# Combining row minima and row sums of attention with an operand per partition on VectorE

## The chip, the cores and the metric

The kernel runs on one core of a Trainium2 chip. The metric is the device time of one execution in microseconds (us); lower is better. Before the change the median of three runs is 3795.2 us (3794.46 to 3797.17).

The core's engines are called by short names: PE is TensorE (matrix products), DVE is VectorE, ACT is ScalarE, POOL is GpSimd, SP is SyncE, whose queue issues nearly all the DMAs. SBUF is the on-chip working memory of 128 partitions, PSUM the memory that PE writes its products to.

## The reference, cut to what matters

Four images of 384 channels and 32 x 32 pixels pass through two layers in fp32. The first is a group normalisation, a selective state-space scan in four directions (16 states for each channel and direction), a layer normalisation and a GELU, added to the image. The second sees the image as 1024 tokens of 384 channels: causal attention with one head, and then a mixture of four experts, of which each token uses two. The change lies in the softmax of the attention:

```python
q = jnp.einsum('btc,ch->bth', x, Wq)
k = jnp.einsum('btc,ch->bth', x, Wk)
v = jnp.einsum('btc,ch->bth', x, Wv)
wei = jnp.einsum('bth,bsh->bts', q, k) * scale
wei = jnp.where(causal, wei, -jnp.inf)
wei = jax.nn.softmax(wei, axis=-1)
out = jnp.einsum('bts,bsh->bth', wei, v)
```

## The kernel before, in words

**Scans.** The scan of an image is cut into 192 units (768 in all, L558 to L571). A unit has 32 channels with 4 states each on the 128 partitions and the 1024 pixels along the free dimension. It takes an exponential `da` on ACT (`decay`, L551), a product `v` on DVE (`front`, L558: `du` and `bc`, both in SBUF, into PSUM), a scan on DVE (`middle`, L564: `da` in SBUF and `v` in PSUM, into `h`), and a product on POOL (`back`, L571: `h` times `bc`, all in SBUF). After every fourth unit PE sums the states (`row`, L596).

**The order of the work.** The kernel is one Python loop over ticks, one unit a tick, which writes the instructions into each engine's queue in a fixed order. In tick t it calls, in this order: `decay` of unit t+2, the deferred functions that are due, `front` of unit t, `back` of unit t-1, the deferred functions of the kind "inner", `middle` (the scan) of unit t, `row`, the fetches, the preparation of the next image and a step of the image before, which is in attention or in the experts. `back` is given a dependence on the `front` of the same tick, so that POOL's product starts once that product of DVE is done, and lies beside the scan.

**Attention.** It runs for image b while the scans of image b+1 go on; for the last image nothing is scanned beside it. For each block i of 128 tokens (8 blocks in an image), `scores` (L925, and L930 for the causal mask) computes the negated scores of the 128 tokens against all tokens up to the block's end on PE. A row of up to 512 scores lies in one PSUM bank. A longer row (i of 4 to 7) has two parts in two banks.

`softmax` is deferred to the "inner" place of a later tick, between `front` and the scan on DVE. It takes the minimum of each part into a column of the small tile `nb` (L939, 48 in all). If there are two parts, it combines their minima into `nb[:, 0:1]` (L941, 16 in all, 4 an image). ACT then takes the exponentials of each part with that minimum as bias, and adds them up into `nb[:, 2:3]` and `nb[:, 3:4]` (L943). `normalise` comes in the next tick, among the functions that are due, ahead of `front`: with two parts it adds the two sums (L953, 16 in all), takes the reciprocal (L954) and lets ACT scale the row (L955). After that, `turn` transposes the row on PE (L970) and copies it with ACT (L887), and `values` multiplies it with the values (L988, L991) and copies the result (L1003).

Other lines that the text speaks of: L339 and L340 in `groupnorm` scale three means and three variances per partition with `tensor_scalar` and a constant, from SBUF to SBUF; L371 normalises 1024 pixels with `tensor_scalar` and two operands per partition, the second of which L368 has just written; L1216 in the experts is a `scalar_tensor_tensor` on DVE with one tensor in PSUM, one in SBUF and an operand per partition in SBUF; L1074 in `gates` adds a constant to four sums.

Of the kernel before, what the change touches and what calls it, by code (L numbers as in the profile page):

```python
# [10 lines left out]
ALU = mybir.AluOpType  # L11
# [38 lines left out]
def hybrid_kernel(  # L50
# [22 lines left out]
    nc = tc.nc  # L73
# [41 lines left out]
    def defer(ticks, f, where=due):  # L115
        where.setdefault(clock[0] + ticks, []).append(f)
# [752 lines left out]
    def attention(b, yb, fx0):  # L869
# [49 lines left out]
        def scores(i):  # L919
            ss = []  # L920
            for o in range(0, (i + 1) * P, 512):
                e = min((i + 1) * P, o + 512)
                ps = yield from banks.take(f"ss_{b}_{i}_{o}")
                for c in range(M):
                    nc.tensor.matmul(  # L925
                        ps[:, : e - o], qt[:, c, i * P : (i + 1) * P], xn[:, c, o:e],
                        start=(c == 0), stop=(c == M - 1 and e <= i * P),
                    )
                if e > i * P:
                    nc.tensor.matmul(ps[:, e - o - P : e - o], ident, causal, start=False, stop=True)  # L930
                ss.append((o, e, ps[:, : e - o]))
                yield "pe", 2.6 * (e - o) / 512
            pr = prs[i] = yield from slots.take(f"pr_{b}_{i}", P, L)
            defer(1, lambda: softmax(i, ss, pr), inner)

        def softmax(i, ss, pr):
            nb = sm.tile([P, 4], F32, tag="nb", name=f"nb_{b}_{i}")
            for n, (o, e, ps) in enumerate(ss):
                nc.vector.tensor_reduce(nb[:, n : n + 1], ps, AX.X, ALU.min)  # L939
            if len(ss) == 2:  # L940
                nc.vector.tensor_tensor(nb[:, 0:1], nb[:, 0:1], nb[:, 1:2], ALU.min)  # L941
            for n, (o, e, ps) in enumerate(ss):
                nc.scalar.activation(  # L943
                    pr[:, o:e], ps, AF.Exp, bias=nb[:, 0:1], scale=-1.0,
                    accum_out=nb[:, 2 + n : 3 + n],
                )
                banks.give(f"ss_{b}_{i}_{o}")
            defer(1, lambda: normalise(i, nb, len(ss)))

        def normalise(i, nb, n):  # L950
            wd = (i + 1) * P
            if n == 2:
                nc.vector.tensor_add(nb[:, 2:3], nb[:, 2:3], nb[:, 3:4])  # L953
            nc.vector.reciprocal(nb[:, 2:3], nb[:, 2:3])  # L954
            nc.scalar.activation(prs[i][:, :wd], prs[i][:, :wd], AF.Copy, scale=nb[:, 2:3])  # L955

# [442 lines left out]
```

## Time and profile before

| | |
|---|---|
| median of three runs | 3795.2 us (3794.46 to 3797.17) |
| profiled execution, its own time | 3795.0 us |
| span of the profile | 3793.2 us |
| mean granted clock of PE | 0.927 |
| PE busy | 3366.5 us, 89% of the span |
| DVE busy | 2964.4 us, 78% |
| ACT busy | 2089.9 us, 55% |
| POOL busy | 1815.1 us, 48% |

The profile is that of one execution. Each engine's busy time counts from an instruction's start to its end as the profiler saw them, so that a wait after the start counts as busy. The granted clock is the share of its full clock that PE was given. In a timeline a row has the start in us from the span's start, the duration in us, the engine, the line of the kernel, the operation, what is written and read by the program's names, the shape per instruction and the count; in brackets stands how long the engine was idle before it, and what ended that. A row that counts more than one instruction merges them, and its duration is then that of the whole stretch. The chain of work that ended last is followed back from the end of the span: at each step to what released the instruction, or to the one ahead of it on its engine.

The work of one image takes about a quarter of the span, shifted so that scans of one image lie beside attention and experts of the one before. The 16 instructions of L941 lie at 821 to 859 us, 1659 to 1704, 2481 to 2520 and 3229 to 3255, four in each stretch. In the last stretch POOL has no work.

### The profile page before, as it was taken

What the parts mean: (1) busy time and instruction counts of PE and PEld (TensorE: products, weight loads), DVE (VectorE), ACT (ScalarE), POOL (GpSimd) and SP (SyncE); (2) the same over time, 40 slices, a digit from 0 to 9 for tenths busy, and PEclk for the clock granted to TensorE, in tenths of its full rate; (3) what the DMA queues carried; (4) which work ended last, traced back from release to release, by engine and by line L of the source; (5) the groups of instructions that cost most, each with busy time, mean ns of one, the idle gap of its engine ahead of it and who ended that gap; (6) DMA issues with size and microseconds to landing.
All of it is one profiled execution on the core that took longest, in us unless ns stands there. A gap on an engine that the chain in (4) does not pass through costs nothing.

```text
span 3793.2 us, 34275 instructions
## 1 busy us (share of the span) xinstructions
PE 3366.5 (89%) x11543; PEld 1518.3 (40%) x11543; DVE 2964.4 (78%) x2084; ACT 2089.9 (55%) x2767; POOL 1815.1 (48%) x776
## 2 busy tenths in 40 slices
PE   4666666689999999799999999889999999999999
PEld 1333333245333334345333343354343434644444
DVE  6899899998889999989998999999999982210000
ACT  5888888555656656556655555455554552422121
POOL 2777777554455556445555565455665550000000
PEclk7767877799999999898999999899999999999999
DMA  6655655635576767336666565345656551222321
GB/s 207 218 209 219 220 199 208 230 122 184 191 245 208 255 205 251 140 136 225 215 221 223 197 212 185 143 167 195 215 194 237 180 182 38 91 78 80 96 83 53
DMA packets 407983, 678.80 MB, mean 179 GB/s; under 512 B 33488, under 2 KB 280576, under 8 KB 407808
## 3 DMA queue, kind: packets, MB, share of 16 engines
q1 hardware_dynamic: 401600, 676.22, 52.0%
q8 instruction: 91, 1.49, 0.2%
q10 hardware_dynamic: 6208, 0.39, 0.1%
q14 instruction: 84, 0.69, 0.1%
HBM read 604.57 MB, written 71.96 MB: 178 GB/s over the span
## 4 chain that ended last, share of the span: by engine, by line
DVE 42%; PE 40%; ACT 7%; issue 6%; DMA 3%; POOL 1%; DVEq 0%; SPq 0%; POOLq 0%; ACTq 0%
DVE h L564 25%; PE ph L1182 13%; PE fy L1207 13%; DVE v L558 12%; PE y L596 4%; ACT da L551 2%; PE ss L925 2%; PE pq L896 2%; PE pv L907 2%; PE v L841 1%; PE pxd L391 1%; ACT st L819 1%; DVE du L438 1%; DMA du<-dts 1%; PE po L991 1%
## 5 line engine op out<-in xcount | busy, mean ns | idle before, releaser
L571 POOL TENSOR_TENSOR h<-h,bc 128x1024 f32<-128x1024 f32 x768 | 1814.0, 2366 | 1308.6 <-DVE v L558 1142.8
L564 DVE TENSOR_TENSOR_SCAN h<-da,v 128x1024 f32<-128x1024 f32 x768 | 1750.5, 2284 | 104.4 <-PE v L841 29.7
L551 ACT ACTIVATE da<-dt,a 128x1024 f32<-128x1024 f32 x768 | 883.3, 1156 | 923.7 <-DVE h L564 887.2
L1182 PE MATMUL ph<-fx,w 128*128 128x512 f32 x2304 | 1024.8, 601 | 6.5 <-ACT dt L430 2.3
L1207 PE MATMUL fy<-ht,w 128*128 128x512 f32 x2304 | 1021.2, 600 | 1.5 <-ACT dt L430 0.9
L558 DVE TENSOR_TENSOR v<-du,bc 128x1024 f32<-128x1024 f32 x678 | 841.7, 1241 | 38.8 <-DMA du<-dts 21.7
L1182 PEld LDWEIGHTS ph<-fx,w 128*128 128x128 f32 x2304 | 434.9, 192 | 583.4 <-issue 528.9
L1207 PEld LDWEIGHTS fy<-ht,w 128*128 128x128 f32 x2304 | 436.8, 192 | 574.9 <-issue 552.2
L596 PE MATMUL y<-h,sel 128*32 128x512 f32 x3072 | 493.8, 661 | 101.4 <-POOL h L571 101.3
L1167 ACT ACTIVATE ht<-ph,b1s 128x512 f32<-128x512 f32 x384 | 257.2, 678 | 459.5 <-PE ph L1182 459.1
L1216 DVE SCALAR_TENSOR_TENSOR fy<-fy,b2s,tw 128x512 f32<-128x512 f32 x96 | 72.4, 754 | 425.8 <-PE fy L1207 425.8
L596 PEld LDWEIGHTS y<-h,sel 128*32 128x32 f32 x3072 | 97.4, 116 | 412.2 <-issue 219.8
L841 PE MATMUL v<-ident,st 128*128 128x128 f32 x720 | 143.1, 364 | 110.6 <-DVE h L564 110.6
L819 ACT ACTIVATE st<-turn,bt 128x128 f32<-128x128 f32 x736 | 213.6, 532 | 0.1
L841 PEld LDWEIGHTS v<-ident,st 128*128 128x128 f32 x720 | 115.4, 189 | 155.6 <-DVE h L564 78.3
L1171 ACT ACTIVATE ht<-ht 128x3072 f32<-128x3072 f32 x64 | 176.9, 2763 | 0.8
L551 ACT ACT_TABLE_LOAD x108 | 138.6, 1283 | 13.8 <-DMA dt<-dts 11.9
L991 PE MATMUL po<-pt,vt 128*128 128x256 f32 x480 | 105.4, 368 | 9.4 <-ACT pt L887 9.4
L424 PE MATMUL pdt<-xd,wdt 12*128 12x512 f32 x184 | 81.0, 762 | 34.8 <-ACT dt L430 19.4
L925 PE MATMUL ss<-axn,qt 128*128 128x512 f32 (+3 forms) x288 | 106.1, 514 | 0.8 <-ACT pr L943 0.5
L991 PEld LDWEIGHTS po<-pt,vt 128*128 128x128 f32 x480 | 93.1, 195 | 24.9 <-ACT pt L887 12.0
L939 DVE TENSOR_REDUCE nb<-ss 128x1 f32<-128x512 f32 (+3 forms) x48 | 26.1, 554 | 78.8 <-PE ss L930 63.5
(200 smaller groups left out, 1661.7 us busy)
## 6 DMA issues: line engine op xcount, KB each, us to landing
bc<-rows SPq DMA_DIRECT2D x384, 512.0 KB, 4.9
w<-in_w SPq DMA_DIRECT2D x384, 384.0 KB, 6.1
dt<-dts SPq DMA_DIRECT2D x192, 512.0 KB, 3.8
du<-dts SPq DMA_DIRECT2D x192, 512.0 KB, 6.7
dts<-dt SPq DMA_DIRECT2D x48, 512.0 KB, 5.3
dts<-du SPq DMA_DIRECT2D x48, 512.0 KB, 3.8
fx<-t2d SPq DMA_DIRECT2D x12, 768.0 KB, 5.3
tw<-mkd SPq DMA_DIRECT2D x32, 256.0 KB, 6.3
```

Of the source, the lines that this page charges most:

```text
L551: nc.scalar.activation(u["da"], spread["dt4", n], AF.Exp, scale=a4[:, g, u["q"] : u["q"] + 1])
L558: return nc.vector.tensor_tensor(u["v"], spread["du4", n], spread["bc", n][:, 0, :], ALU.mult)
L564: nc.vector.tensor_tensor_scan(u["h"][:, ::step], u["da"][:, ::step], u["v"][:, ::step], 0.0, op0=ALU.mult, op1=ALU.add,)
L571: product = nc.gpsimd.tensor_tensor(h, h, spread["bc", n][:, 1, :], ALU.mult)
L596: nc.tensor.matmul(y, sel, h, start=first, stop=last, tile_position=(0, jj * DJ))
L819: nc.scalar.activation(st[:, 4 * h + t, :].rearrange("p (d i) -> p i d", i=NI)[:, i, :], ps[h][:, t * P : (t + 1) * P], AF.Copy, scale=bt[ ...
L841: nc.tensor.transpose(u["v"][:, t * P : (t + 1) * P], st[:, t, u["j"] * P : (u["j"] + 1) * P], ident)
L925: nc.tensor.matmul(ps[:, : e - o], qt[:, c, i * P : (i + 1) * P], xn[:, c, o:e], start=(c == 0), stop=(c == M - 1 and e <= i * P),)
L991: nc.tensor.matmul(pv[:, o:], vt[:, j, m * P : (m + 1) * P], pts[step][j // 4][:, j % 4, o:], start=False, stop=(j == nj - 1),)
L1167: nc.scalar.activation(ht[:, f, :], ps, AF.Identity, bias=bias)
L1182: nc.tensor.matmul(ps, tiles[n][:, c, (f % 2) * P : (f % 2 + 1) * P], xns[h][:, c, :], start=(c == 0), stop=(c == M - 1),)
L1207: nc.tensor.matmul(pss[m], tiles[n][:, f, :], hts[fh][:, f, :], start=(fh == 0 and f == 0), stop=(fh == 1 and f == FH - 1),)
```

## The change

In `softmax`, the tensor_tensor that takes the smaller of two minima becomes a tensor_scalar: its one tensor is the first minimum, and the second comes in as an operand per partition. In `normalise`, the tensor_tensor that adds the two sums becomes a tensor_scalar in the same way. Operands, result and the place in the order stay the same.

```diff
             if len(ss) == 2:
-                nc.vector.tensor_tensor(nb[:, 0:1], nb[:, 0:1], nb[:, 1:2], ALU.min)
+                nc.vector.tensor_scalar_min(nb[:, 0:1], nb[:, 0:1], nb[:, 1:2])
...
             if n == 2:
-                nc.vector.tensor_add(nb[:, 2:3], nb[:, 2:3], nb[:, 3:4])
+                nc.vector.tensor_scalar_add(nb[:, 2:3], nb[:, 2:3], nb[:, 3:4])
```

## The prediction

> **What bounds the kernel now.** I read the chain of work that ended last first, to see which engine a saved microsecond must come from.
>
> ```profile
> DVE 42%; PE 40%; ACT 7%; issue 6%; DMA 3%; POOL 1%; DVEq 0%; SPq 0%; POOLq 0%; ACTq 0%
> ```
>
> VectorE (DVE) and TensorE (PE) carry the end in turn. From 800 to 3160 us, where attention and experts of one image lie beside the scans of the next, DVE is 92% busy (2176.6 of 2360 us) and PE 95%, so a stall of either is likely to count. Second, the groups of instructions by form, for the two lines that are changed (columns: instructions, busy us and mean ns, idle before).
>
> ```profile
> L941 DVE TENSOR_TENSOR nb<-nb 128x1 f32<-128x1 f32 x16 | 11.4, 712 | 0.6
> ...
> L953 DVE TENSOR_TENSOR nb<-nb 128x1 f32<-128x1 f32 x16 | 2.2, 140 | 5.4 <-ACT pr L943 5.4
> ```
>
> The same shape of operation costs 140 ns at L953 and 712 ns at L941. The single instructions of L941 run from 159 to 1711 ns with a median of 182, so a few long ones make the mean. Third, the timeline around one long one (start, us, engine, line).
>
> ```profile
> 839.03 2.34 POOL L571 TENSOR_TENSOR h<-h,bc 128x1024 f32<-128x1024 f32 x1 [1.26 <-DVE v L558]
> ...
> 839.96 1.44 DVE L941 TENSOR_TENSOR nb<-nb 128x1 f32<-128x1 f32 x1
> 841.32 2.27 DVE L564 TENSOR_TENSOR_SCAN h<-da,v 128x1024 f32<-128x1024 f32 x1
> ```
>
> GpSimd's (POOL's) product ends at 839.03 + 2.34 = 841.37; L941 ends at 841.40. In all seven instances of 0.67 us and more (at 830.02, 839.96, 1659.29, 1684.69, 2481.16, 2491.08 and 2501.05) it ends within 0.03 us of the end of the product under way. One comparison per partition takes 160 ns where no product is under way, so most of those 1.44 us are a wait for POOL, booked as busy. Fourth, is that wait on the path? The chain in order of time, same place:
>
> ```profile
> 838.87 1.07 DVE nb L939 x2
> 839.93 0.02 issue
> 839.96 1.44 DVE nb L941
> 841.40 2.20 DVE h L564
> ```
>
> The chain passes through it, as through the other six. Nothing hides it.
>
> **What the Trainium skill says.** "GPSIMD Engine Reference", section "Key points", says that POOL shares its SBUF interfaces with VectorE, and that it contends with DVE instructions in a 2-port performance mode or with two SBUF inputs. The trace agrees for two inputs: L941 reads both from SBUF and waits, while L1216 (one SBUF tensor, one in PSUM, one operand per partition from SBUF) takes 0.75 us at 1001.29 inside a product that runs from 1000.36 to 1002.72, its usual time of 754 ns. So an operand per partition, as such, doesn't wait. "VectorE: DVE Perf Modes", section "The perf-mode tier table", gives fp32 tensor_scalar in SBUF the 2x mode, which uses both ports. The trace agrees: L371 handles 1024 elements in 811 ns, where L558 takes 1241 for the same width. "Vector Engine (DVE) Microarchitecture Reference", section 5.1, ties that mode to SBUF operands whose outermost dimension over one is even, or equal on both sides. What one element per partition does it doesn't say, and no row of this trace shows a tensor_scalar of one element. "TensorE: Matmul & The Clock Gate", section "What's actually happening", says that PE falls to half clock after an idle window of about 3.4 us; the trace agrees, with a granted clock of 0.50 from 2508.6 to 2512.2, after 3.40 us of idle.
>
> **The change, part by part.**
>
> Removed: 16 tensor_tensor at L941, 11.4 us. Added: 16 tensor_scalar with an operand per partition, in the same place of the same queue. No DMA, tile or wait on another engine is added, and POOL's and SP's queues are untouched. Undisturbed instances of L941 take 159 to 163 ns. The nearest rows for the new form are L339 and L340 (tensor_scalar, 128x3), 136 to 154 ns undisturbed, and L1074 (128x4), 170 ns. So the bare operation changes by -0.02 to +0.01 us, and 16 of them by -0.4 to +0.2 us. I take 0. Reading as an operand per partition what the instruction in front has just written adds no gap that I can see: L371 starts 0.04 us after L368, which writes its operand, as L941 starts 0.03 us after L939.
>
> The wait is the open cost. 11.4 us less 16 x 0.160 = 2.6 us leaves **8.8 us**. At one end the new form doesn't contend, and all 8.8 us are gone; at the other it contends as before, and nothing is. The row that argues for the latter is L339, where it meets the end of a product:
>
> ```profile
> 1415.47 2.35 POOL L571 TENSOR_TENSOR h<-h,bc 128x1024 f32<-128x1024 f32 x1 [1.34 <-DVE v L558]
> 1417.63 0.20 DVE L339 TENSOR_SCALAR gn_mc<-gn_mc 128x3 f32<-128x3 f32 x1
> ```
>
> It takes 205 instead of 136 ns and ends at 1417.83, as the product ends (1417.82); so a tensor_scalar of three elements does wait. What one element does rests on whether a single element is split over two ports. There is nothing to split, so I take, narrowly, that it isn't and that the wait goes.
>
> L953 -> tensor_scalar_add: its 16 instances take 126 to 160 ns, none meets a product, the new form costs the same by the rows above; 0. Its cover is that it comes right behind a scan, when the product that ran beside that scan is over. With L941 faster, the product still started before the scan and ends before it (831.57 against about 832.4 at the first place), so the cover stays. Without it, one sum could wait up to 2.35 us.
>
> What is late next, if the 8.8 us go? Behind L941 on DVE stands the scan L564; on ACT the exponentials L943 wait for it, and behind them `da`, the copies and PE's transposes. At the first image (1.41 + 1.28 = 2.7 us) the chain comes to PE here (PE's timeline, idle before it in brackets):
>
> ```profile
> 849.24 0.48 PE L970 MATMUL tp<-ident,pr 128*128 128x128 f32 x1 [4.53 <-ACT yb L1003]
> ```
>
> PE sat idle for 4.53 us, more than 2.7, so it takes the whole gain. At the second image, 0.5 us meet idle of 0.88 (1666.85), and 1.28 us meet 3.40 (1692.28). At the third, 1.55 + 1.48 + 1.28 = 4.3 us meet 3.40 at 2508.63; PE's work ahead of that can itself move up by its own waits of 0.33 and 0.56, so some 4.2 pass. That makes 2.7 + 0.5 + 1.3 + 4.2 = 8.7 us. Afterwards all engines have moved alike, so the shift stays to the end; the last image's four instances (3229 to 3254) have no product beside them, and change by 0.
>
> A second gain comes from PE's clock. The gaps at 849, 1692 and 2508 are followed by about 6 us at half clock (12 matmuls of L925 take 8.0 us at 849.7, and 5.15 at 3248 where the clock is full), so 3 us each. In the shorter gaps (about 2.9, 2.6 and under 0.5 us) the fall is likely avoided at the third and about evenly open at the other two. But DVE waits for those scores by only 1.23, 1.03 and 1.11 us (before L939 at 857.99, 1702.71 and 2518.78), and no more than that can be had: 0.5 x 1.2 + 0.5 x 1.0 + 0.9 x 1.1 = 2.1 us. Small losses, where PE has less slack than I see, I put at 0.8 us.
>
> Sum against the profiled execution: span 3793.2 - 8.7 - 2.1 + 0.8 = 3783.2 us; with the 1.8 us around the span (3795.0 - 3793.2) 3785.0. Its time stands 0.2 us under the median of the three runs, 3795.2, which is less than their spread of 2.7.
>
> **The rivals.**
>
> The wait stays. The single element runs in the two-port mode after all, and L941 ends with the product, as before. For it: L339. Against it: one element has no second half. Nothing moves: 3795.0 us, 3793.5 to 3797.
>
> The wait goes, and PE's clock takes it back; this one ends slower. DVE frees the scores earlier, PE runs ahead, and gaps that are now just short of a fall grow past it: 2.21 us before 1708.55, 2.21 before 2524.61, 2.79 before 2539.15. Each fall costs about 3 us (6 us at half clock). It decides from the third fall that is new: 3795.0 - 8.7 + 3 x 3 = 3795.3, and with a fourth 3798.3. Against it: the gaps after the waits shrink, since PE waits for DVE there, and the stages after them move as a whole.
>
> The change does not do what it says: if both forms came out as the same instruction, the profile would show TENSOR_TENSOR at L941 again, and the time is that of the first rival. I count it there.
>
> **How the numbers follow.** The wait goes: 0.52, 3785 us, own range 3781 to 3789. The wait stays: 0.41, 3795. Clock takes it back: 0.07, about 3798. The first two hold most of the chance, so the range reaches from 3782 to 3797. A measurement of this kernel can tell about 0.2%, that is 7.6 us, from no change; the line is 3787.6. Four fifths of the first case lie below it: 0.42 faster. The rest of the first case (0.10), the second and 0.04 of the third are within 0.2%: 0.55. Slower by more: 0.03, the part of the third with more falls than the four counted.
>
> **What would show it.** Right: a TENSOR_SCALAR at L941 with 16 instances near 160 ns, the longest under 0.25 us, though a product runs; DVE's busy time down by about 9 us; the idle before PE's L970 (849) and L596 (1692, 2508) shorter. Wrong in the second way: the longest instance is still about 1.7 us and ends with a product. Wrong in the third: L941 is short, and PE's granted clock falls in stretches where it is full now. My forecast fails if one element does take both ports.

## The result, and the profile after

The changed kernel takes 3781.2 us (median of 8 runs, 3779.65 to 3789.62), against 3796.2 (8 runs, 3790.32 to 3803.41, the three shown first among them) for the kernel before. The ratio is 0.9968 with a 95% interval of 0.9959 to 0.9977: 12.1 us less, between 8.7 and 15.6. The two medians lie 15.0 us apart, which is within that interval. The median of the changed kernel lies 0.8 us under the forecast's range.

The profiled execution of the changed kernel has a span of 3777.9 us. The chain's shares first:

```profile
DVE 41%; PE 40%; ACT 7%; issue 7%; DMA 3%; POOL 1%; DVEq 0%; SPq 0%; POOLq 0%; ACTq 0%
```

DVE and PE still carry the end in turn; no other engine has become the bound. The two changed lines in the groups by form:

```profile
L941 DVE TENSOR_SCALAR nb<-nb 128x1 f32<-128x1 f32 x16 | 3.4, 214 | 0.6
...
L953 DVE TENSOR_SCALAR nb<-nb 128x1 f32<-128x1 f32 x16 | 3.2, 200 | 5.8 <-ACT pr L943 5.8
```

L941 went from 11.4 to 3.4 us and is now even: its 16 instances take 213 to 215 ns. L953 went from 2.2 to 3.2 us. DVE's busy time fell from 2964.4 to 2956.2 us. The timeline at the place that the prediction showed:

```profile
837.49 2.35 POOL L571 TENSOR_TENSOR h<-h,bc 128x1024 f32<-128x1024 f32 x1 [1.26 <-DVE v L558]
838.41 0.21 DVE L941 TENSOR_SCALAR nb<-nb 128x1 f32<-128x1 f32 x1
838.54 2.28 DVE L564 TENSOR_TENSOR_SCAN h<-da,v 128x1024 f32<-128x1024 f32 x1
```

The product runs until 839.84, and the minimum is done at 838.62 all the same; the scan starts 1.3 us before the product ends. On the chain in order of time the piece shrank from 1.44 to 0.21 us, with the same neighbours:

```profile
837.32 1.07 DVE nb L939 x2
838.39 0.03 issue
838.41 0.21 DVE nb L941
838.62 2.19 DVE h L564
```

**Where the time came from.** I measured three attention stages by DVE's scans, counted from 1 to 768: from the start of scan 223 to that of 230, of 413 to 425, and of 607 to 617. They hold all the waits. Each figure is from one execution, the profiled one. In the kernel before they last 30.9, 59.4 and 48.0 us; in the changed one 28.5, 55.8 and 42.9. That is 2.4 + 3.6 + 5.1 = 11.1 us less. The two profiled spans differ by 15.3. The other 4.2 us lie outside the three stages, where the changed kernel spends 3650.6 us and the kernel before 3654.9. Of the kernels below, those that keep the waits spend 3654.5 to 3661.9 us there, and those that lose them 3653.1 to 3662.7: single executions differ by more than 4.2 us there, so this part isn't shown to be the change's. 11.1 us fit the ratio's 12.1.

### The profile page after: what moved, and what is told of

Read it like the earlier page. It is cut to its first block, busy times and chain, and to the rows that moved or that the text cites. A ratio compares the mean times of both kernels' runs of the same rounds, so it can differ in the third digit from the quotient of the medians.

```text
span 3777.9 us, 34275 instructions
## 1 busy us (share of the span) xinstructions
PE 3355.5 (89%) x11543; PEld 1511.6 (40%) x11543; DVE 2956.2 (78%) x2084; ACT 2089.8 (55%) x2767; POOL 1815.2 (48%) x776
## 4 chain that ended last, share of the span: by engine, by line
DVE 41%; PE 40%; ACT 7%; issue 7%; DMA 3%; POOL 1%; DVEq 0%; SPq 0%; POOLq 0%; ACTq 0%
DVE h L564 25%; PE ph L1182 14%; PE fy L1207 13%; DVE v L558 13%; PE y L596 4%; ACT da L551 2%; PE pq L896 2%; PE pv L907 2%; PE v L841 1%; DMA du<-dts 1%; PE ss L925 1%; PE pxd L391 1%; PE po L991 1%; DVE du L438 1%; DVE fy L1216 1%
## 5 line engine op out<-in xcount | busy, mean ns | idle before, releaser
L551 ACT ACT_TABLE_LOAD x108 | 138.6, 1283 | 13.3 <-DMA dt<-dts 11.4
```

The lines of the kernel that those rows point to most:

```text
L551: nc.scalar.activation(u["da"], spread["dt4", n], AF.Exp, scale=a4[:, g, u["q"] : u["q"] + 1])
```

## Experiments

The three stages as above, and the ratio to the kernel before, for all kernels:

| kernel | stage 1, us | stage 2, us | stage 3, us | ratio (95% interval) |
|---|---|---|---|---|
| before | 30.9 | 59.4 | 48.0 | 1 |
| changed | 28.5 | 55.8 | 42.9 | 0.9968 (0.9959 to 0.9977) |
| min_only | 28.3 | 56.7 | 42.7 | 0.9967 (0.9954 to 0.9979) |
| sum_only | 31.0 | 59.4 | 48.2 | 1.0000 (0.9992 to 1.0008) |
| two_elements | 30.9 | 59.2 | 48.1 | 0.9998 (0.9990 to 1.0006) |
| min_then_idle | 30.9 | 58.4 | 48.1 | 1.0001 (0.9993 to 1.0009) |
| min_then_free | 28.5 | 57.0 | 43.2 | 0.9973 (0.9965 to 0.9981) |
| psum_second | 28.2 | 57.4 | 43.7 | 0.9976 (0.9968 to 0.9984) |
| third_image | 30.9 | 58.7 | 42.7 | 0.9988 (0.9982 to 0.9995) |
| const_sum | 28.3 | 56.7 | 42.7 | one run, 3786.2 us |
| filled_gap | 30.9 | 61.7 | 51.6 | 1.0018 (1.0010 to 1.0025) |
| min_filled | 28.3 | 61.9 | 42.7 | 0.9987 (0.9980 to 0.9995) |
| filled_zero | 30.9 | 59.1 | 48.0 | 1.0000 (0.9992 to 1.0009) |
| min_filled_zero | 28.3 | 55.3 | 42.7 | 0.9966 (0.9954 to 0.9978) |

My theory: a tensor_tensor with both inputs in SBUF can't run while POOL's product does, a tensor_scalar of a single element can, and the scan behind it carries the gain. Rivals: the new form as such is faster, wherever it stands; the gain comes from the exponentials, not from the scan; a value per partition never waits, whatever the number of elements.

**Each half alone: min_only and sum_only.**

```diff
 min_only
-                nc.vector.tensor_tensor(nb[:, 0:1], nb[:, 0:1], nb[:, 1:2], ALU.min)
+                nc.vector.tensor_scalar_min(nb[:, 0:1], nb[:, 0:1], nb[:, 1:2])
 sum_only
-                nc.vector.tensor_add(nb[:, 2:3], nb[:, 2:3], nb[:, 3:4])
+                nc.vector.tensor_scalar_add(nb[:, 2:3], nb[:, 2:3], nb[:, 3:4])
```

> Only the minimum (L941) takes its second value per partition; the sum stays a tensor_tensor. If the wait for GpSimd's product at L941 is the whole cause, L941 takes 0.21 us in all 16 instances and the time is that of the full change, ratio 0.997 to the kernel before, less about 0.05 us for each of 16 sums. If the sum has a share in the gain, the ratio lies between 0.997 and 1.

> Only the sum (L953) takes its second value per partition. If L941's wait is the cause, nothing is gained: L941 keeps its seven instances of 0.6 to 1.7 us, each sum takes 0.19 instead of 0.13 us, and the time is 0 to 1 us above the kernel before, ratio 1.000. If the new form itself is what helps, it falls by some microseconds.

The minimum alone gives the whole gain; the sum alone gives none. With the sum alone, the groups by form read:

```profile
L941 DVE TENSOR_TENSOR nb<-nb 128x1 f32<-128x1 f32 x16 | 11.6, 723 | 0.5
...
L953 DVE TENSOR_SCALAR nb<-nb 128x1 f32<-128x1 f32 x16 | 3.1, 195 | 5.4 <-ACT pr L943 5.4
```

The sum takes 195 instead of 140 ns, and no more is to be had, since nothing waits at L953. The new form as such is slower, not faster: the first rival falls.

**One element or two: two_elements.** The minimum is taken over both columns, so the second column comes out as it was.

```diff
-                nc.vector.tensor_tensor(nb[:, 0:1], nb[:, 0:1], nb[:, 1:2], ALU.min)
+                nc.vector.tensor_scalar_min(nb[:, 0:2], nb[:, 0:2], nb[:, 1:2])
```

> The minimum takes its second value per partition, but over both columns of the tile (two elements per partition; the second comes out unchanged). The sum stays. If one element escapes because it can't be split over two ports, two elements are split, and L941 waits for the product again: up to 1.7 us, ratio 1.000. If a value per partition never waits, L941 takes 0.21 us and the ratio is 0.997.

```profile
842.82 2.34 POOL L571 TENSOR_TENSOR h<-h,bc 128x1024 f32<-128x1024 f32 x1 [1.26 <-DVE v L558]
843.74 1.44 DVE L941 TENSOR_SCALAR nb<-nb 128x2 f32<-128x2 f32 x1
845.10 2.27 DVE L564 TENSOR_TENSOR_SCAN h<-da,v 128x1024 f32<-128x1024 f32 x1
```

The timeline at the same place shows the wait again: it ends at 845.18, and the product at 845.16. The operation, the operand per partition and the place are those of the changed kernel; only the second element is new. So the wait goes because of the single element, not because of the operand per partition alone. This is the step that the prediction left to a guess. The reading, which no run shows directly, is that one element isn't handled in the mode that needs both ports. It agrees with the Trainium skill, "Vector Engine (DVE) Microarchitecture Reference", section 5.1: by the rule there, two elements from SBUF to SBUF with one source take the mode with both ports, as an even count does; of one element the page says nothing.

**The scan or the exponentials, which both wait for the minimum: min_then_idle and min_then_free.** An instruction whose result nobody reads stands behind the new minimum and ahead of the scan, once in each form.

```diff
+    junk = const.tile([P, 1], F32, tag="junk", name="junk")
...
-                nc.vector.tensor_tensor(nb[:, 0:1], nb[:, 0:1], nb[:, 1:2], ALU.min)
+                nc.vector.tensor_scalar_min(nb[:, 0:1], nb[:, 0:1], nb[:, 1:2])
+                nc.vector.tensor_tensor(junk, eps, eps, ALU.min)      # min_then_idle
+                nc.vector.tensor_scalar_min(junk, eps, eps)           # min_then_free
```

> The minimum as in the changed kernel, and behind it a tensor_tensor of one element with two SBUF inputs, whose result nobody reads. It should wait for the product in the place of L941, up to 1.7 us, and hold the scan behind it, but not ScalarE's exponentials. If the scan's delay carries the loss, the time is that of the kernel before (ratio 1.000); if the exponentials' delay carries it, that of the changed kernel (0.997).

> As the kernel with an idle tensor_tensor behind the new minimum, but that instruction too is a tensor_scalar of one element with its second value per partition. It is the control for the bare cost of one more instruction in that place: 16 x 0.2 us at most, so a ratio of 0.997 to 0.998. If one more instruction on DVE in this place is by itself what loses the gain, it is 1.000.

The timeline of min_then_idle (its lines count one further, two behind the edit):

```profile
841.23 2.35 POOL L572 TENSOR_TENSOR h<-h,bc 128x1024 f32<-128x1024 f32 x1 [1.26 <-DVE v L559]
842.15 0.21 DVE L942 TENSOR_SCALAR nb<-nb 128x1 f32<-128x1 f32 x1
842.28 1.32 DVE L943 TENSOR_TENSOR junk<-eps 128x1 f32<-128x1 f32 x1
842.40 0.69 ACT L945 ACTIVATE pr<-ss,nb 128x512 f32<-128x512 f32 x1 [1.46 <-DVE nb L942]
...
843.52 2.27 DVE L565 TENSOR_TENSOR_SCAN h<-da,v 128x1024 f32<-128x1024 f32 x1
```

The exponentials start at 842.40, right behind the minimum, as in the changed kernel. The idle instruction ends at 843.60, and the product at 843.58. The scan behind it starts at 843.52; here as in the kernel before and in the changed one, its start lies 0.08 us ahead of the end of the instruction in front. The gain is gone: ratio 1.0001. In the other form the instruction costs 204 ns, and the ratio stays at 0.9973. So what counts is the scan's delay. The wait needs no dependence on anything: both inputs are one constant tile.

**Another way around the wait: psum_second.** The tensor_tensor stays; for blocks 4 to 6 the second minimum goes to the free last column of its PSUM bank.

```diff
             for n, (o, e, ps) in enumerate(ss):
-                nc.vector.tensor_reduce(nb[:, n : n + 1], ps, AX.X, ALU.min)
+                low = nb[:, n : n + 1] if n == 0 or spare_ is None else spare_
+                nc.vector.tensor_reduce(low, ps, AX.X, ALU.min)
             if len(ss) == 2:
-                nc.vector.tensor_tensor(nb[:, 0:1], nb[:, 0:1], nb[:, 1:2], ALU.min)
+                nc.vector.tensor_tensor(nb[:, 0:1], nb[:, 0:1], low, ALU.min)
```

`spare_` is column 511 of the second part's bank for blocks 4 to 6, and None for block 7, whose bank is full.

> The minimum stays a tensor_tensor, but for the blocks 4 to 6 of an image the second part's minimum is written to the free last column of its PSUM bank, so that only one of the two inputs lies in SBUF. If two SBUF inputs are what waits, the twelve instances of blocks 4 to 6 take about 0.2 us beside a product and the ratio is about 0.997, a little behind the changed kernel [...]. If any tensor_tensor waits, it stays at 1.000.

The groups by form (the first line is block 7, the second blocks 4 to 6):

```profile
L943 DVE TENSOR_TENSOR nb<-nb 128x1 f32<-128x1 f32 x4 | 2.8, 708 | 0.1
...
L943 DVE TENSOR_TENSOR nb<-nb,ss 128x1 f32<-128x1 f32 x12 | 1.9, 155 | 0.4
```

With one input in PSUM none of the twelve waits, so two SBUF inputs are the cause. They take 155 ns, no more than the undisturbed 159 to 163 with both inputs in SBUF. But the ratio is only 0.9976, and the stages 2 and 3 gain less than with the new form. The reason is in the first line: the minimum of block 7, which didn't wait in the kernel before, now does. It takes 1.09 us in the second stage and 1.30 in the third, and in each of them the last two scans of the stage (423 to 425, 615 to 617) take 11.2 us instead of min_only's 10.1. The wait has moved.

**One stage alone: third_image.** The new minimum for the third image, the old one for the others (`if b == 2`).

> Only the third image's four minima take their second value per partition. By the working of the prediction this stage gains 4.2 us from the waits and about 1.0 us from PE's clock, and the other stages nothing: the stretch of the third attention is 5.2 us shorter, and the ratio is about 0.9986. If the shift didn't stay to the end, or the gain lay elsewhere, the ratio would be 1.000.

The third stage takes 42.7 us, 5.3 less, and the first one is as before; the second is 0.7 shorter, within what it varies by among kernels with its waits (58.4 to 59.4; why it varies is seen further down). The ratio is 0.9988, where 5.3 of 3796 us are 0.9986. The gain stays to the end.

**What the operand per partition costs: const_sum.** The minimum in the new form, and the sum with a constant.

```diff
-                nc.vector.tensor_add(nb[:, 2:3], nb[:, 2:3], nb[:, 3:4])
+                nc.vector.tensor_scalar_add(nb[:, 2:3], nb[:, 2:3], 1.0)
```

> The minimum as in the changed kernel; the sum adds a constant in place of the second sum (which is left out, so the weights of long rows are not normalised rightly). If the value per partition is what makes the new form take 0.19 to 0.21 us, L953 takes about 0.13 us here; if it is tensor_scalar as such, 0.19 us.

```profile
L953 DVE TENSOR_SCALAR nb<-nb 128x1 f32<-128x1 f32 x16 | 2.2, 138 | 3.4 <-ACT pr L943 3.4
```

By the groups by form, the sum takes 138 ns with a constant and 195 to 200 with an operand per partition (sum_only and the changed kernel): the operand costs about 60 ns an instruction.

**The share of PE's clock: filled_gap and min_filled, then filled_zero and min_filled_zero.** In the second and third stage PE is idle for 3.4 us until POOL's last product is there, and its clock falls to half for 6.8 us, from 0.8 and 1.4 us before PE starts again. Three matmuls in that gap should keep it up. In the first attempt they wrote to a bank for scores:

```diff
+                if n in (419, 611) and half == 0 and jj == NJ - 1 and banks.ready():
+                    fill = bank("fill")
+                    for _ in range(3):
+                        nc.tensor.matmul(fill, ident, ybs[b - 1][:, 0, :512], start=True, stop=True)
                 nc.tensor.matmul(
                     y, sel, h, start=first, stop=last, tile_position=(0, jj * DJ)
                 )
```

(The lines are written out here from a helper of one line. 419 and 611 are units counted from 0; min_filled has the new minimum and 419 alone.)

> The kernel before, with three matmuls of 512 columns whose result nobody reads put into PE's idle time ahead of the last product of the second and third attention stage (3.4 us idle before), so that PE's clock should not fall; the waits at L941 stay. If PE's clock has a share of its own in the gain, the half-clock stretches of 6.8 us go, and scores of block 7 come 3 us earlier; DVE then takes their minima some 1.0 us earlier in each of the two stages. Two outcomes: either the stages are 1.0 us shorter each (58.4 and 47.0 us from 59.4 and 48.0), or L941 of block 7, which in the kernel before starts 0.1 us before a product ends, now meets that product and waits about 1.1 us, and the stages stay as long as they were. I expect the second: the clock's gain is only to be had with the new form.

> Only the minimum in its new form, and the same three idle matmuls in the gap of the second attention stage alone (in the third the clock doesn't fall any more). If the clock's fall there still costs, the stage of 56.7 us with the minimum alone gets up to 1 us shorter, and the time is at most that of the changed kernel (ratio 0.9965); if DVE is not waiting for those scores, it stays at 56.7 us.

The attempt missed: the bank still held values that ACT had not copied yet, as the timeline of filled_gap shows (a matmul counts as two there, so that three are x6).

```profile
2513.00 4.74 PE L574 MATMUL fill<-yb,ident 128*128 128x512 f32 x6 [4.93 <-ACT yb L1003]
```

The gap grew to 4.93 us, and everything behind the filling came later; both kernels say nothing on the clock. In the second attempt the three matmuls have weights of zero and add into the rows that are being written anyway, from the unit ahead, which is there:

```diff
+    none = const.tile([P, DJ], F32, tag="none", name="none")
+    nc.vector.memset(none, 0.0)
...
+                if (n, half, jj) in ((419, 0, 3), (611, 0, 3)):
+                    for _ in range(3):
+                        nc.tensor.matmul(
+                            y, none, before, start=False, stop=False,
+                            tile_position=(0, jj * DJ),
+                        )
+                before = h
                 nc.tensor.matmul(
                     y, sel, h, start=first, stop=last, tile_position=(0, jj * DJ)
                 )
```

> The kernel before with its waits, and the gap filled without a bank: three more sums of the third unit's states with weights of zero, added into the rows that PE is about to write in any case, ahead of the matmul that waits for GpSimd's last product of the second and third attention stage. They need nothing that isn't there, so they should run in the 3.4 us of idle time and keep PE's clock up. If the clock has a share of its own, either the stages get 1.0 us shorter each (58.4 and 47.0 us), or L941 of block 7 comes 1 us earlier, meets a product and waits for it, and the stages stay at 59.4 and 48.0. I expect the second.

> Only the minimum in its new form, and the same filling in the second stage alone. If the clock's fall there still costs, the stage gets up to 1 us shorter than the 56.7 us with the minimum alone, and the time is 0 to 1 us under that kernel's; if DVE doesn't wait for those scores, nothing changes.

PE's timeline of filled_zero in the third stage (lines behind the edit count nine further, those of scans and products two):

```profile
2511.73 1.90 PE L605 MATMUL y<-h,sel 128*32 128x512 f32 x10 [1.67 <-POOL h L573]
2513.56 5.42 PE L934 MATMUL ss<-axn,qt 128*128 128x512 f32 x12
```

The first row takes 1.90 us, where the kernel before needs 3.62 for the same ten, and the scores 5.42 instead of 6.34. The clock no longer falls in this stage. Yet the stage lasts 48.0 us as before. Here is why, in filled_zero's DVE and POOL:

```profile
2520.09 1.28 DVE L948 TENSOR_REDUCE nb<-ss 128x1 f32<-128x512 f32 x2
2520.35 2.34 POOL L573 TENSOR_TENSOR h<-h,bc 128x1024 f32<-128x1024 f32 x1 [1.34 <-DVE v L560]
2521.41 1.30 DVE L950 TENSOR_TENSOR nb<-nb 128x1 f32<-128x1 f32 x1
2522.64 2.27 DVE L566 TENSOR_TENSOR_SCAN h<-da,v 128x1024 f32<-128x1024 f32 x1
```

and the same block in the kernel before:

```profile
2517.25 2.35 POOL L571 TENSOR_TENSOR h<-h,bc 128x1024 f32<-128x1024 f32 x1 [1.35 <-DVE v L558]
2518.78 0.69 DVE L939 TENSOR_REDUCE nb<-ss 128x1 f32<-128x512 f32 x1 [1.11 <-PE ss L930]
2519.51 0.16 DVE L941 TENSOR_TENSOR nb<-nb 128x1 f32<-128x1 f32 x1
2519.59 2.29 DVE L564 TENSOR_TENSOR_SCAN h<-da,v 128x1024 f32<-128x1024 f32 x1
```

Before, DVE idled 1.11 us for the scores and came to the minimum 0.09 us before the product's end. With the scores in time it doesn't idle, reaches the minimum 1.3 us before the product ends, and waits there instead. The product sets the time either way. So with the old form nothing is gained at block 7 when PE's clock stays up.

In min_filled_zero the second stage takes 55.3 us, 1.4 less than with the minimum alone. But the filling isn't the reason. From scan 423, just ahead of block 7's minimum, to scan 425 both kernels take 10.1 us: in min_only, too, DVE finds block 7's scores ready, though PE's clock is at half for 3.4 us behind the gap. The 1.4 us lie at scan 418, at block 5, some 13 us ahead of the filling. In min_only:

```profile
1661.37 5.83 PE L925 MATMUL ss<-axn,qt 128*128 128x512 f32 x12
1665.94 0.69 DVE L939 TENSOR_REDUCE nb<-ss 128x1 f32<-128x512 f32 x1 [1.16 <-PE ss L925]
```

and in min_filled_zero:

```profile
1662.39 4.39 PE L934 MATMUL ss<-axn,qt 128*128 128x512 f32 x12
1665.73 0.68 DVE L948 TENSOR_REDUCE nb<-ss 128x1 f32<-128x512 f32 x1
```

In min_only PE's clock is at half from 1662.0 to 1665.4, and DVE waits for the scores; in min_filled_zero and in the changed kernel it is full there. This fall comes and goes whatever the form: of the kernels that wait in this stage, before, sum_only, two_elements and filled_zero have it, and min_then_idle, third_image and filled_gap don't; of those that don't wait, the changed kernel and min_filled_zero alone lack it. Where it is missing in a kernel that waits, block 5's minimum meets the product (it takes 0.93 us in third_image), and scan 418 comes 0.4 to 0.7 us earlier and not 1.4. As a whole min_filled_zero is no faster than the two others (0.9966 against 0.9967 and 0.9968).

## Why the prediction was right, step by step

- **The wait at L941 is for POOL, on the path, and goes.** Shown: min_only has the gain, sum_only none; two_elements and min_then_idle bring the wait and the loss back, psum_second takes it away by another road.
- **One element doesn't wait.** The guess that the whole forecast stood on (0.52 to 0.41). two_elements decides it at the same place, with the same operation: two elements wait, one doesn't. That one isn't split over two ports fits this, and remains the reading.
- **The bare operation costs the same.** Wrong in size. The rows I took, L339, L340 and L1074, add or multiply a constant; with a constant the sum takes 138 ns here too. The new form takes 214 ns at L941 where I had 160, and 200 at L953 where I had 140. That is 16 x 0.054 + 16 x 0.06 = 1.8 us of DVE time, which I had put at 0. The 8.8 us of wait were right: 11.4 - 3.4 = 8.0, plus the 0.9 by which the bare minima grew.
- **PE takes the gain.** Right as a whole, stage by stage less so: predicted were 2.7, 1.8 and 4.2 us and 0.6, 0.5 and 1.0 from the clock, so 3.3, 2.3 and 5.2; measured are 2.4, 3.6 (2.7 with the minimum alone) and 5.1. With the minimum alone the three stages give 10.6 us: 8.4 up to block 7, from the seven waits (8.7 predicted), and 0, 1.1 and 1.2 at block 7, where no minimum waited before. The changed kernel's 11.1 are these 10.6, plus 1.4 for the fall at block 5 that is missing in its one execution, less 0.9, of which the operands of the twelve sums make up some 0.7 (an estimate, 12 x 0.06). That the forecast of 10.0 us in all comes so close is in part luck, since neither of the last two was in it.
- **PE's clock.** The gaps in the changed kernel are 3.96, 3.45 and 1.41 us, where I had 2.9, 2.6 and under 0.5: PE's work ahead of a gap moved up too, since some of its own waits went. PE's timeline has two of them:

```profile
846.52 0.47 PE L970 MATMUL tp<-ident,pr 128*128 128x128 f32 x1 [3.96 <-ACT yb L1003]
...
2494.50 1.90 PE L596 MATMUL y<-h,sel 128*32 128x512 f32 x10 [1.41 <-POOL h L571]
```

  So the fall stays in the first stage (6.8 us at half clock as before, 5.0 of them inside the stage where it was 4.2), is halved in the second (3.4 instead of 6.8) and is gone in the third, as forecast there. The length of a gap doesn't decide alone, as the prediction took it to: in the kernel before, the clock fell 2.6 and 2.0 us into the two gaps of 3.40 of the second and third stage, stayed full over the one of 2.79 before 2539.15, and fell at 1667.57 with no gap over 0.9 us in the 12 us ahead of it.
- **What I didn't see:** that faster scores would have sent block 7 into the product, as filled_zero and psum_second show. The new form takes away those waits as well, which a count of the waits in the profile of before can't show. In the changed kernel ten instances of L941 start with 0.6 us or more of a product to go, not seven, and those of block 7 in the second and third stage with 1.3 each.
- **The rivals.** The wait doesn't stay. New falls of the clock don't take the gain back: outside the three stages PE is at half clock for 536 to 565 us in the kernels that keep the waits, and for 525 to 589 in those that lose them. One of the gaps that were taken for just short of a fall, the 2.21 us before 1708.55, already had one in the kernel before (1708.53 to 1711.94).
- **The range** was cut too close below: the first case's own lower end was 3781, and I had given part of it away. The median lies at 3781.2; by the ratio, from the 3795.2 us of the runs shown first, it is 3783.1, where the sum gave 3785.0.

What stays open is how much of the 2.3 us at block 7 of the second and third stage is owed to PE's clock. filled_zero shows that with the old form a clock that stays up brings nothing there, and min_filled_zero that with the new form the 3.4 us at half clock that are left in the second stage cost nothing. But no run has the new form with the whole fall of 6.8 us and the gap as it was. In the first stage the clock falls as before, and block 7 gains nothing.

## What to carry to other kernels

A tiny instruction whose busy time varies by ten, as L941's did from 0.16 to 1.71 us, may be waiting for something, even if the profile books it as work: set its end against the ends on the other engines. Before counting on a wait that goes, look for the instruction that today is late for another reason; it may step into the same wait. Take the price of a form from a row with the same kind of operand, not only the same operation. And when a stage gets shorter in one execution, find the place in it: a gain that lies ahead of the edit isn't the edit's.

## What the runs showed of the hardware

A tensor_tensor of one element with both inputs in SBUF, begun with more than its own 0.16 us of a POOL product on SBUF to go, ended 13 to 19 ns after that product, up to 1.7 us later; with one input in PSUM it took 155 ns. At L941's place, a tensor_scalar of one element with an operand per partition, from SBUF to SBUF, took 212 to 216 ns beside the product or not; with two elements it took 228 to 230 ns undisturbed, and ended 24 to 27 ns after the product. An operand per partition cost about 60 ns over a constant (195 to 200 against 138 ns at the sum). PE's half-clock stretches at the gaps in the second and third stage lasted 3.4 or 6.8 us, and a fall of 3.4 us at block 5 was there in some kernels' executions and missing in others, whatever the form.
